# First image ahead of the weights, and a last projection split by heads, in an attention block on one core

## The chip, the cores and the metric

One NeuronCore of one Trainium2 chip runs the whole program. The metric is the device time of one execution in microseconds (us). Every run used here has a granted TensorE clock of 0.997 or more.

Engines are called as the profile calls them: PE is TensorE, PEld its weight loads, DVE VectorE, ACT ScalarE, POOL GpSimd, SPq and ACTq the queues that issue transfers. `rstd` is the reciprocal of the norm's standard deviation, one small power on GpSimd per image; it serves as a mark for the images.

## The reference, cut to what matters

Sixteen images of 512 channels and 32 x 32 = 1024 positions, in fp32, go through a group norm, a four-head attention over the positions, and a projection with a residual.

```python
def _L0_conv_ref(x, norm_gamma, norm_beta, qkv_w, qkv_b, proj_w, proj_b):
    NUM_HEADS, NUM_GROUPS, EPS = 4, 8, 1e-05
    b, c, h, w = x.shape            # 16, 512, 32, 32
    ...
    xn = ((xg - mu) * jax.lax.rsqrt(var + EPS)).reshape(b, c, h, w)
    xn = xn * norm_gamma[:, None, None] + norm_beta[:, None, None]
    qkv = jnp.einsum('oc,bchw->bohw', qkv_w, xn) + qkv_b[:, None, None]
    q, k, v = jnp.split(qkv, 3, axis=1)
    ...
    attn = jax.nn.softmax(jnp.einsum('bhnd,bhmd->bhnm', q, k) * scale, axis=-1)
    out = jnp.einsum('bhnm,bhmd->bhnd', attn, v)
    ...
    out = jnp.einsum('oc,bchw->bohw', proj_w, out) + proj_b[:, None, None]
    return x + out
```

## The kernel before

The three matrix products with weights (q and k, v, projection) are each done as 2 x 2 blocks with seven products in place of eight (Strassen's scheme in Winograd's form). For that, sums of weight blocks are formed once, and sums of image blocks (or of the heads' outputs) per image. `t1` to `t4` are the image sums, `s1` to `s4` the weight sums; s1, s2, s4 have buffers of their own, s3 overwrites a21, t1 overwrites b12.

```python
FACTORS = {
    1: ("a11", "b11"), 2: ("a12", "b21"), 3: ("s4", "b22"), 4: ("a22", "t4"),
    5: ("s1", "t1"), 6: ("s2", "t2"), 7: ("s3", "t3"),
}

def sums_of_a(eng, a, cols):          # weights
    for k in range(KC):
        def at(n):
            return a[n][k][:, cols]
        eng.tensor_add(at("s1"), at("a21"), at("a22"))
        eng.tensor_sub(at("s3"), at("a11"), at("a21"))
        eng.tensor_sub(at("s2"), at("s1"), at("a11"))
        eng.tensor_sub(at("s4"), at("a12"), at("s2"))

def sums_of_b(eng, b):                # image, or heads' outputs
    for k in range(KC):
        eng.tensor_sub(b["t3"][k], b["b22"][k], b["b12"][k])
        eng.tensor_sub(b["t1"][k], b["b12"][k], b["b11"][k])
        eng.tensor_sub(b["t2"][k], b["b22"][k], b["t1"][k])
        eng.tensor_sub(b["t4"][k], b["b21"][k], b["t2"][k])
```

One quad of products, `quad`, is a list of seven units, run in the order p1, p6, p2, p7, p5, p4, p3. Each unit is four matmul instructions and an eviction. Two accumulator banks (`ps_a`, `bufs=2`) serve them all.

```python
        def p6():
            mm(bank(6), 6, True)
            u[2] = upool.tile([P, HALF], F32, tag="u2", bufs=2, name=f"{name}_u2")
            nc.vector.tensor_add(u[2], banks[6], u["p1"])
        ...
        return [p1, p6, p2, p7, p5, p4, p3]
```

In the projection the residual is loaded into one of four `y` buffers (`ypool`, `bufs=4`), and for three of the four output blocks GpSimd adds it after the eviction:

```python
        def plus(which, half):
            def f(acc, u):
                t = upool.tile([P, HALF], F32, tag="yu", bufs=2, name=f"yu_{b}_{o}_{which}_{half}")
                nc.vector.scalar_tensor_tensor(t, acc, bias(which), u, ALU.add, ALU.add)
                nc.gpsimd.tensor_add(res[which, half], res[which, half], t)
                store(which, half)
            return f
```

The main loop has 8 steps per head. Beside the scores and weighted sums of a step, it emits what the plan of that head holds; in the fourth head that is the next image's norm, its image sums, the q/k quad of its first head and both v quads:

```python
        elif b + 1 < B:
            spread(plan, [lambda c=c: normalise(b + 1, c) for c in range(NCC)], 0, 1)
            plan[0].append(lambda: x_sums(b + 1))
            spread(
                plan, qk_units(b + 1, 0) + v_units(b + 1, 0) + v_units(b + 1, 1), 1, NB
            )
```

The start, with the v bias carried through the projection (32 one-column instructions), and the end:

```python
    load_x(0)
    ...                                   # wqk on the sync queue, wv and wp on ScalarE's
    stats_group(0)
    for half in range(NH2):
        for c in range(NCC):
            normalise(0, c, half)
    x_sums(0)
    sums_of_a(nc.vector, wqk, ts(0, P))
    sums_of_a(nc.gpsimd, wv, slice(0, HC))
    sums_of_a(nc.gpsimd, wqk, slice(P, C))
    for o in range(NCC):
        ...                               # acc[:, 0:1] += block.T @ vb_sb[:, c], added to projb_sb
    sums_of_a(nc.gpsimd, wp, slice(0, HC))
    for u in qk_units(0, 0) + v_units(0, 0) + v_units(0, 1):
        u()
    ...                                   # the main loop
    divide(B - 1, HEADS - 1)
    o_sums(B - 1)
    for u in proj_units(B - 1, 0) + proj_units(B - 1, 1):
        u()
```

The division needs one row of reciprocal totals on all partitions: `row` goes out to memory and `rinv` comes back broadcast, one transfer after the other.

## Time and profile before

| | before |
|---|---|
| time, median of the first 3 runs | 3400.59 us (3399.67 to 3401.64) |
| profiled span | 3400.3 us |
| TensorE busy | 3342.2 us, 98% |
| first q/k product, first v product | 35.62, 52.26 us |
| one image to the next (rstd to rstd), mean of 14 | 209.21 us |
| first projection product of the last image to the end of the span | 39.83 us |
| of it, until the last head's division starts | 7.63 us |

A profile row gives start, busy time, engine, line, operation, `output<-inputs`, shapes, count, and in brackets the idle time before it with what ended it. Busy time alone does not show where this program can be made faster, because TensorE is busy nearly everywhere; the gaps at the start, once per image and at the end do.

### The profile page before, as it was taken

Reading aid. Unit: us, or ns where it says so; the run is one execution under the profiler, and the core shown is the slowest. Engines: PE = TensorE matmul, PEld = TensorE weight load, DVE = VectorE, ACT = ScalarE, POOL = GpSimd, SP = SyncE. Lnnn points to the kernel's source line nnn. Section 1 sums busy time; section 2 is a strip of 40 time slices with the busy share of each in tenths; the row PEclk is TensorE's granted clock in tenths of the full one; section 3 lists DMA queues with packets and bytes.
Section 4 is the critical chain, followed back from the end, with each engine's and each line's share of the span. In section 5 each row is a group of like instructions: output and inputs, shape, how many; then the busy total and the mean of one; then the engine's idle time right before and its main releaser. Section 6 shows DMA issues by size and latency. Waiting matters only on the chain.

```text
span 3400.3 us, 22944 instructions
## 1 busy us (share of the span) xinstructions
PE 3342.2 (98%) x8674; PEld 1635.7 (48%) x8674; DVE 1641.3 (48%) x2408; ACT 790.8 (23%) x869; POOL 172.4 (5%) x140
## 2 busy tenths in 40 slices
PE   6999999999999999999999999999999999999998
PEld 4454454544545445454454545445454454544543
DVE  4454644546345464453544545454454544546444
ACT  1222222222122121221222212222222212222221
POOL 2000000000000000000000000000000000000000
PEclk9999999999999999999999999999999999999999
DMA  2001101011020110101111011110101101011011
GB/s 87 13 31 43 56 13 68 19 59 41 18 76 13 56 37 28 65 13 56 38 38 56 13 56 37 40 53 13 62 31 44 50 13 62 31 44 56 13 56 51
DMA packets 62660, 140.24 MB, mean 41 GB/s; under 512 B 10320, under 2 KB 12368, under 8 KB 62544
## 3 DMA queue, kind: packets, MB, share of 16 engines
q1 hardware_dynamic: 59232, 135.56, 11.4%
q10 hardware_dynamic: 3312, 3.16, 0.3%
q8 instruction: 70, 1.15, 0.1%
q14 instruction: 46, 0.38, 0.0%
HBM read 104.87 MB, written 33.82 MB: 41 GB/s over the span
## 4 chain that ended last, share of the span: by engine, by line
PE 63%; issue 29%; DVE 5%; POOL 2%; DMA 1%; ACT 0%; SPq 0%; POOLq 0%; DVEq 0%
PE po L489 15%; PE s L445 14%; PE qk L319 13%; PE pp L386 11%; PE v L352 11%; DVE x L71 1%; POOL rstd L63 1%; DVE xt L156 1%; DVE tt L462 1%; POOL y L417 1%; DVE part L464 1%; DMA wqk_a<-in_qkv_wT 0%; ACT p L450 0%; DVE yu L416 0%; DVE tot L455 0%
## 5 line engine op out<-in xcount | busy, mean ns | idle before, releaser
L450 ACT ACTIVATE p<-s 128x1024 f32<-128x1024 f32 x512 | 524.4, 1024 | 2031.4 <-PE s L445 2029.1
L489 PE MATMUL po<-p,v 128*128 128x512 f32 x2048 | 972.1, 593 | 0.0
L445 PE MATMUL s<-qk,qk 128*128 128x512 f32 x2048 | 964.8, 592 | 0.0
L455 DVE TENSOR_TENSOR tot<-tot,p 128x1024 f32<-128x1024 f32 x384 | 477.4, 1243 | 931.6 <-ACT p L450 931.0
L445 PEld LDWEIGHTS s<-qk,qk 128*128 128x128 f32 x2048 | 389.1, 190 | 489.4 <-issue 482.2
L489 PEld LDWEIGHTS po<-p,v 128*128 128x128 f32 x2048 | 386.8, 190 | 443.4 <-issue 388.8
L319 PE MATMUL qk<-x,wqk_a 128*128 128x512 f32 x512 | 248.4, 603 | 0.7 <-ACT qk_p L283 0.7
L319 PE MATMUL qk<-x,wqk_s 128*128 128x512 f32 x512 | 243.0, 592 | 0.0
L319 PE MATMUL qk<-xt,wqk_a 128*128 128x512 f32 x512 | 240.6, 592 | 0.0
L417 POOL TENSOR_TENSOR y<-y,yu 128x512 f32<-128x512 f32 x96 | 121.0, 1267 | 2232.2 <-DVE yu L416 2232.2
L498 DVE TENSOR_TENSOR o<-o,rinv 128x1024 f32<-128x1024 f32 x64 | 78.2, 1223 | 199.9 <-ACT o L495 139.4
L319 PEld LDWEIGHTS qk<-x,wqk_a 128*128 128x128 f32 x512 | 96.8, 192 | 130.1 <-issue 97.3
L336 DVE SCALAR_TENSOR_TENSOR qk<-qk,qkb_sb,qk_u 128x512 f32<-128x512 f32 x192 | 143.4, 747 | 28.7 <-PE qk L319 28.7
L319 PEld LDWEIGHTS qk<-xt,wqk_a 128*128 128x128 f32 x512 | 97.3, 190 | 122.5 <-issue 122.5
L319 PEld LDWEIGHTS qk<-x,wqk_s 128*128 128x128 f32 x512 | 97.3, 190 | 122.5 <-issue 122.0
L319 PE MATMUL qk<-xt,wqk_s 128*128 128x512 f32 x256 | 127.3, 610 | 17.9 <-DVE xt L158 17.9
L386 PE MATMUL pp<-o,wp_a 128*128 128x512 f32 x256 | 122.9, 602 | 5.1 <-DVE o L498 5.1
L386 PE MATMUL pp<-ot,wp_a 128*128 128x512 f32 x256 | 122.7, 602 | 0.0
L386 PE MATMUL pp<-o,wp_s 128*128 128x512 f32 x256 | 121.9, 598 | 0.0
L352 PE MATMUL v<-wv_a,xt 128*128 128x256 f32 x512 | 121.0, 379 | 0.0
L352 PE MATMUL v<-wv_a,x 128*128 128x256 f32 x512 | 120.9, 379 | 0.0
L352 PE MATMUL v<-wv_s,x 128*128 128x256 f32 x512 | 120.9, 379 | 0.0
(93 smaller groups left out, 2043.5 us busy)
## 6 DMA issues: line engine op xcount, KB each, us to landing
y<-in_x SPq DMA_DIRECT2D x128, 256.0 KB, 2.6
rinv<-row SPq DMA_DIRECT2D x64, 512.0 KB, 3.6
out_y<-y SPq DMA_DIRECT2D x128, 256.0 KB, 2.0
x<-in_x SPq DMA_DIRECT2D x62, 512.0 KB, 3.8
wqk_a<-in_qkv_wT SPq DMA_DIRECT2D x8, 256.0 KB, 4.5
x<-in_x ACTq DMA_DIRECT2D x2, 512.0 KB, 6.9
wv_a<-in_qkv_wT ACTq DMA_DIRECT2D x8, 128.0 KB, 4.1
wp_a<-in_proj_wT ACTq DMA_DIRECT2D x8, 128.0 KB, 4.1
```

Source lines behind the costliest of these rows:

```text
L63: nc.gpsimd.tensor_tensor(rstd, ve, self.neghalf, ALU.pow)
L71: nc.vector.tensor_scalar(xn, x, mu[:, c : c + 1], sc[:, c : c + 1], ALU.subtract, ALU.mult)
L319: nc.tensor.matmul(acc, wqk[wn][k][:, ts(h, P)], xb[b][xn][k], start=(first and k == 0), stop=(k == KC - 1), skip_group_check=True,)
L336: return lambda acc, u: nc.vector.scalar_tensor_tensor(dst(which, half), acc, bias(which), u, ALU.add, ALU.add)
L352: nc.tensor.matmul(acc[:, ts(g, HC)], xb[b][xn][k][:, ts(2 * jj + g, P)], wv[wn][k], start=(first and g == 0 and k == 0), stop=(k == KC - ...
L386: nc.tensor.matmul(acc, wp[wn][k][:, ts(o, P)], ob[b][on][k], start=(first and k == 0), stop=(k == KC - 1), skip_group_check=True,)
L417: nc.gpsimd.tensor_add(res[which, half], res[which, half], t)
L445: nc.tensor.matmul(sc[:, ts(half, HALF)], ks[b, h][:, ts(j, P)], qs[b, h][:, ts(half, HALF)], start=True, stop=True,)
L450: nc.scalar.activation(ps[s], sc, AF.Exp, scale=SCALE)
L455: nc.vector.tensor_add(tot[b, h], tot[b, h], ps[s])
L489: nc.tensor.matmul(po[b, h][:, ts(half, HALF)], vs[b, h // 2][:, h % 2, j, :], p[:, ts(half, HALF)], start=(j == 0), stop=(j == NB - 1),)
L498: nc.vector.tensor_mul(os_[b, h], os_[b, h], rinv.pop((b, h)))
```

## The change

Its intent is threefold. At the start, the first image must not wait for weight sums or bias products: GpSimd gets no work before the norm's power, weights come in one queue with the first head's columns first, small "warm" products keep TensorE active until the image is there, and the bias products move into the second head. In the middle, the image sums are reordered so that t2 is ready early, and the next image's units begin one step later. At the end, the products that don't need the last head run before its division, with four extra accumulator banks taken from the scores; the residual is added to `u` on VectorE, ahead of the last eviction. A new rule makes residual loads wait for the image's last eviction (`last_eviction`).

```diff
-def sums_of_b(eng, b):
-    for k in range(KC):
-        eng.tensor_sub(b["t3"][k], b["b22"][k], b["b12"][k])
-        eng.tensor_sub(b["t1"][k], b["b12"][k], b["b11"][k])
-        eng.tensor_sub(b["t2"][k], b["b22"][k], b["t1"][k])
-        eng.tensor_sub(b["t4"][k], b["b21"][k], b["t2"][k])
+def sums_of_b(eng, b, rows=(1, 2), chunks=range(KC)):
+    def sub(o, i, j):
+        for k in chunks:
+            eng.tensor_sub(b[o][k], b[i][k], b[j][k])
+    if 1 in rows:
+        sub("t1", "b12", "b11")
+    if 2 in rows:
+        sub("t2", "b22", "t1")
+        sub("t3", "t2", "b11")
+        sub("t4", "b21", "t2")
@@ loads (cut) @@
+    nc.scalar.activation(primer, ones, AF.Exp)
...
+    load_first()          # wqk, columns 0 to 127
+    load_v()
+    load_rest()           # wqk, the others
+    load_p()
@@ quad (cut): any order of units, banks may come from elsewhere @@
-            u["p1"] = upool.tile([P, HALF], F32, tag="p1", name=f"{name}_p1")
+            u["p1"] = upool.tile([P, HALF], F32, tag="p1", bufs=2, name=f"{name}_p1")
...
+            results.get("u2", nothing)(u[2])
@@ projection @@
+            tc.add_manual_dep(
+                dma.ins, last_eviction[b].ins.name,
+                mybir.DependencyInfo(mybir.DependencyClass.Sync, mybir.DependencyReason.DATA),
+                reason="residual",
+            )
...
+        def add(u, *places):
+            for at in places:
+                eng.tensor_add(res[at], res[at], u)
+        def put(which, half):
+            def f(acc, u=None):
+                t = res.pop((which, half))
+                bias = projb_sb[:, o + 2 * which : o + 2 * which + 1]
+                nc.vector.scalar_tensor_tensor(t, acc, bias, t, ALU.add, ALU.add)
+                nc.sync.dma_start(out[b, ts(o + 2 * which, P), ts(half, HALF)], t)
             return f
@@ plan of the fourth head @@
-                plan, qk_units(b + 1, 0) + v_units(b + 1, 0) + v_units(b + 1, 1), 1, NB
+                plan, qk_units(b + 1, 0) + v_units(b + 1, 0) + v_units(b + 1, 1), 2, NB
@@ start @@
+    before_power = norm.last
+    warm(9, "warm")
...
-    sums_of_a(nc.vector, wqk, ts(0, P))
-    sums_of_a(nc.gpsimd, wv, slice(0, HC))
-    sums_of_a(nc.gpsimd, wqk, slice(P, C))
...
+    with tc.issue_after(before_power.ins):
+        sums_of_a(nc.vector, wqk, ts(0, P))
+    for u in qk_units(0, 0, order=(1, 2, 6, 7, 5, 4, 3)):
+        u()
+    sums_of_a(nc.vector, wv, slice(0, HC))
+    for u in v_units(0, 0) + v_units(0, 1):
+        u()
@@ end @@
-    divide(B - 1, HEADS - 1)
-    o_sums(B - 1)
-    for u in proj_units(B - 1, 0) + proj_units(B - 1, 1):
+    order = (1, 5, 2, 6, 7, 4, 3)
+    first = proj_units(B - 1, 0, nc.vector, order=order, home={6: home(6, 0), 7: home(6, 1)})
+    second = proj_units(B - 1, 1, nc.vector, order=order, home={1: home(1, 0), 5: home(1, 1)})
+    sums_of_b(nc.vector, ob[B - 1], (1,))
+    for u in first[:1] + second[:1] + first[1:2] + second[1:2]:
+        u()
+    sums_of_b(nc.vector, ob[B - 1], (2,), (0,))
+    divide(B - 1, HEADS - 1)
+    sums_of_b(nc.vector, ob[B - 1], (2,), (1,))
+    for u in first[2:3] + second[2:3] + first[3:] + second[3:]:
         u()
```

More of the change, by code (lines that the diff above doesn't have):

```diff
@@ L60, in group @@
         ve = gn.tile([P, k], F32, tag="ve", name="ve")
-        nc.vector.tensor_scalar_add(ve, pv[:, :k], EPS)
+        self.last = nc.vector.tensor_scalar_add(ve, pv[:, :k], EPS)
         rstd = gn.tile([P, k], F32, tag="rstd", name="rstd")
@@ L202, in fast_path @@
     load_x(0)
+    primer = wpool.tile([BLK, 1], F32, name="primer")
+    nc.vector.memset(ones, 1.0)
+    nc.scalar.activation(primer, ones, AF.Exp)
     nc.vector.memset(avg, 0.0)
@@ L206, in fast_path, with w_tiles @@
     nc.vector.memset(neghalf, -0.5)
-    nc.vector.memset(ones, 1.0)
-    for t, src in ((gamma_sb, gamma), (beta_sb, beta), (qkb_sb, qk_b)):
+    for t, src in (
+        (gamma_sb, gamma), (beta_sb, beta), (qkb_sb, qk_b), (vb_sb, v_b), (projb_sb, proj_b)
+    ):
         nc.scalar.dma_start(t, src)
-    def w_tiles(name, cols, dma, blocks):
+    def w_tiles(name, cols, blocks, parts):
         w = {}
@@ L216, in w_tiles, with load @@
         w["s3"] = w["a21"]
-        for n, src in blocks:
-            for k in range(KC):
-                dma.dma_start(w[n][k], src[ts(k, P), :])
-        return w
+        def load(part):
+            for n, src in blocks:
+                for k in range(KC):
+                    nc.sync.dma_start(w[n][k][:, part], src[ts(k, P), part])
+        return w, [lambda part=part: load(part) for part in parts]
     def blocks_of(first, second):
@@ L226, in blocks_of @@
         ]
-    wqk = w_tiles("wqk", C, nc.sync, blocks_of(qkv_wT[:, 0:C], qkv_wT[:, C : 2 * C]))
-    wv = w_tiles(
-        "wv", HC, nc.scalar,
+    wqk, (load_first, load_rest) = w_tiles(
+        "wqk", C, blocks_of(qkv_wT[:, 0:C], qkv_wT[:, C : 2 * C]), (slice(0, P), slice(P, C))
+    )
+    wv, (load_v,) = w_tiles(
+        "wv", HC,
         blocks_of(qkv_wT[:, 2 * C : 2 * C + HC], qkv_wT[:, 2 * C + HC : 3 * C]),
+        (slice(0, HC),),
     )
-    nc.scalar.dma_start(vb_sb, v_b)
-    nc.scalar.dma_start(projb_sb, proj_b)
-    wp = w_tiles("wp", HC, nc.scalar, blocks_of(proj_wT[:, 0:HC], proj_wT[:, HC:C]))
+    wp, (load_p,) = w_tiles(
+        "wp", HC, blocks_of(proj_wT[:, 0:HC], proj_wT[:, HC:C]), (slice(0, HC),)
+    )
+    load_first()
+    load_v()
+    load_rest()
+    load_p()
     norm = Norm(nc, gn, ps_a, avg, neghalf, gamma_sb, beta_sb, NCC, N)
@@ L268, in x_sums, with quad @@
         sums_of_b(nc.vector, xb[b])
-    def quad(name, mm, results, shape=None):
-        banks = {}
+    def quad(name, mm, results, order=(1, 6, 2, 7, 5, 4, 3), home=None):
+        banks, u = {}, {}
+        nothing = lambda u: None
         def bank(i):
-            banks[i] = ps_a.tile([P, HALF], F32, tag="acc", name=f"{name}_{i}")
+            if home and i in home:
+                banks[i] = home[i]()
+            else:
+                banks[i] = ps_a.tile([P, HALF], F32, tag="acc", name=f"{name}_{i}")
             return banks[i]
@@ L295, in p7 @@
             mm(bank(7), 7, True)
-            u[3] = upool.tile([P, HALF], F32, tag="u3", name=f"{name}_u3")
+            u[3] = upool.tile([P, HALF], F32, tag="u3", bufs=2, name=f"{name}_u3")
             nc.vector.tensor_add(u[3], banks[7], u[2])
+            results.get("u3", nothing)(u[3])
+            if 5 in banks:
+                results["c22"](banks[5], u[3])
         def p5():
             mm(bank(5), 5, True)
-            results["c22"](banks[5], u[3])
+            if 3 in u:
+                results["c22"](banks[5], u[3])
         def p4():
@@ L309, in p3, with qk_units @@
             results["c12"](banks[5], u[2])
-        u = {}
-        return [p1, p6, p2, p7, p5, p4, p3]
-    def qk_units(b, h):
+        units = {1: p1, 2: p2, 3: p3, 4: p4, 5: p5, 6: p6, 7: p7}
+        return [units[i] for i in order]
+    def qk_units(b, h, **kw):
         def mm(acc, i, first):
@@ L342, in qk_units @@
             "c12": plus(0, 1), "c21": plus(1, 0), "c22": plus(1, 1),
-        })
+        }, **kw)
     def v_units(b, jj):
@@ L379, in o_sums, with proj_units @@
         sums_of_b(nc.vector, ob[b])
-    def proj_units(b, o):
+    def proj_units(b, o, eng, **kw):
         def mm(acc, i, first):
@@ L395, in load @@
             t = ypool.tile([P, HALF], F32, tag="y", name=f"y_{b}_{o}_{which}_{half}")
-            nc.sync.dma_start(t, x[b, ts(o + 2 * which, P), ts(half, HALF)])
-            res[which, half] = t
-        def store(which, half):
-            nc.sync.dma_start(
-                out[b, ts(o + 2 * which, P), ts(half, HALF)], res.pop((which, half))
-            )
-        def bias(which):
-            return projb_sb[:, o + 2 * which : o + 2 * which + 1]
-        def c11(acc):
-            nc.vector.scalar_tensor_tensor(
-                res[0, 0], acc, bias(0), res[0, 0], ALU.add, ALU.add
-            )
-            store(0, 0)
-        def plus(which, half):
-            def f(acc, u):
-                t = upool.tile([P, HALF], F32, tag="yu", bufs=2, name=f"yu_{b}_{o}_{which}_{half}")
-                nc.vector.scalar_tensor_tensor(t, acc, bias(which), u, ALU.add, ALU.add)
-                nc.gpsimd.tensor_add(res[which, half], res[which, half], t)
-                store(which, half)
+            dma = nc.sync.dma_start(t, x[b, ts(o + 2 * which, P), ts(half, HALF)])
+            tc.add_manual_dep(
+                dma.ins, last_eviction[b].ins.name,
+                mybir.DependencyInfo(mybir.DependencyClass.Sync, mybir.DependencyReason.DATA),
+                reason="residual",
+            )
+            res[which, half] = t
+        def add(u, *places):
[7 more added lines that the diff above has]
+                nc.sync.dma_start(out[b, ts(o + 2 * which, P), ts(half, HALF)], t)
             return f
         units = quad(f"pp_{b}_{o}", mm, {
-            "c11": c11, "c12": plus(0, 1), "c21": plus(1, 0), "c22": plus(1, 1),
-        })
+            "u2": lambda u: add(u, (0, 1), (1, 0)), "u3": lambda u: add(u, (1, 1)),
+            "c11": put(0, 0), "c12": put(0, 1), "c21": put(1, 0), "c22": put(1, 1),
+        }, **kw)
         first = units[0]
@@ L432, in proj_units @@
         return [with_loads] + units[1:]
-    ps, tot, po, rinv = {}, {}, {}, {}
+    ps, tot, po, rinv, last_eviction = {}, {}, {}, {}, {}
     def where(s):
@@ L494, in weighted_sum @@
             os_[b, h] = opool.tile([P, N], F32, tag="o", name=f"o_{b}_{h}")
-            nc.scalar.copy(os_[b, h], po.pop((b, h)))
+            last_eviction[b] = nc.scalar.copy(os_[b, h], po.pop((b, h)))
     def divide(b, h):
@@ L503, in spread, with bias_of_v @@
             plan[first + i * (last - first) // len(units)].append(u)
+    def bias_of_v(o):
+        acc = ps_a.tile([P, HALF], F32, tag="acc", name=f"pb_{o}")
+        half, oo = divmod(o, 2)
+        for c in range(NCC):
+            block = wp[f"a{half + 1}{c // KC + 1}"][c % KC]
+            nc.tensor.matmul(
+                acc[:, 0:1], block[:, ts(oo, P)], vb_sb[:, c : c + 1],
+                start=(c == 0), stop=(c == NCC - 1),
+            )
+        nc.vector.tensor_add(
+            projb_sb[:, o : o + 1], projb_sb[:, o : o + 1], acc[:, 0:1]
+        )
     def plan_head(b, h):
         plan = [[] for _ in range(NB)]
+        if b == 0 and h < 2:
+            if h == 0:
+                plan[0].append(lambda: sums_of_a(nc.vector, wqk, ts(1, P)))
+                plan[3].append(lambda: sums_of_a(nc.vector, wqk, ts(2, P)))
+            else:
+                plan[0].append(lambda: sums_of_a(nc.vector, wqk, ts(3, P)))
+                spread(plan, [lambda o=o: bias_of_v(o) for o in range(NCC)], 1, 5)
+                plan[6].append(lambda: sums_of_a(nc.vector, wp, slice(0, HC)))
         if h == 0:
@@ L511, in plan_head @@
                 plan[3].append(lambda: o_sums(b - 1))
-                spread(plan, proj_units(b - 1, 0), 4, NB)
+                spread(plan, proj_units(b - 1, 0, nc.gpsimd), 4, NB)
         elif h == 1:
             if b > 0:
-                spread(plan, proj_units(b - 1, 1), 0, 4)
+                spread(plan, proj_units(b - 1, 1, nc.gpsimd), 0, 4)
             spread(plan, qk_units(b, 2), 0, NB)
@@ L526, in plan_head, with warm @@
             spread(
-                plan, qk_units(b + 1, 0) + v_units(b + 1, 0) + v_units(b + 1, 1), 1, NB
+                plan, qk_units(b + 1, 0) + v_units(b + 1, 0) + v_units(b + 1, 1), 2, NB
             )
         return plan
+    def warm(n, name):
+        acc = ps_s.tile([P, N], F32, tag="s", name=name)
+        for _ in range(n):
+            ins = nc.tensor.matmul(acc[:, :P], avg, avg, start=True, stop=True)
+            tc.keep_in_program_order(ins)
     for c in range(NCC):
@@ L537, in fast_path @@
     x_sums(0)
-    sums_of_a(nc.vector, wqk, ts(0, P))
-    sums_of_a(nc.gpsimd, wv, slice(0, HC))
-    sums_of_a(nc.gpsimd, wqk, slice(P, C))
-    for o in range(NCC):
-        acc = ps_a.tile([P, HALF], F32, tag="acc", name=f"pb_{o}")
-        half, oo = divmod(o, 2)
-        for c in range(NCC):
-            block = wp[f"a{half + 1}{c // KC + 1}"][c % KC]
-            nc.tensor.matmul(
-                acc[:, 0:1], block[:, ts(oo, P)], vb_sb[:, c : c + 1],
-                start=(c == 0), stop=(c == NCC - 1),
-            )
-        nc.vector.tensor_add(
-            projb_sb[:, o : o + 1], projb_sb[:, o : o + 1], acc[:, 0:1]
-        )
-    sums_of_a(nc.gpsimd, wp, slice(0, HC))
-    for u in qk_units(0, 0) + v_units(0, 0) + v_units(0, 1):
+    with tc.issue_after(before_power.ins):
[4 more added lines that the diff above has]
+    for u in v_units(0, 0) + v_units(0, 1):
         u()
@@ L582, in fast_path, with home, f @@
     nc.vector.tensor_scalar(flag, fine, -1.0, 1.0, ALU.mult, ALU.add)
+    spare = {}
+    def home(i, half):
+        def f():
+            if i not in spare:
+                spare[i] = ps_s.tile([P, N], F32, tag="s", name=f"spare_{i}")
+            return spare[i][:, ts(half, HALF)]
+        return f
+    ob[B - 1] = halves([os_[B - 1, h] for h in range(HEADS)], "o")
+    order = (1, 5, 2, 6, 7, 4, 3)
[5 more added lines that the diff above has]
+    sums_of_b(nc.vector, ob[B - 1], (2,), (0,))
     divide(B - 1, HEADS - 1)
-    o_sums(B - 1)
-    for u in proj_units(B - 1, 0) + proj_units(B - 1, 1):
+    sums_of_b(nc.vector, ob[B - 1], (2,), (1,))
+    for u in first[2:3] + second[2:3] + first[3:] + second[3:]:
         u()
```

## The prediction

> **What bounds the kernel now.** I read three views in this order. First the page's busy times and its 40 slices, to see how much any change can win.
>
> ```profile
> PE 3342.2 (98%) x8674; PEld 1635.7 (48%) x8674; DVE 1641.3 (48%) x2408; ACT 790.8 (23%) x869; POOL 172.4 (5%) x140
> ...
> PE   6999999999999999999999999999999999999998
> ```
>
> TensorE (PE) is busy 98% of the span, and only the first and the last slice (85 us each) fall below 9 tenths. Part of this is busy time that need not be so long, so I set up a floor from the spacing of instruction starts instead. In the timeline of the middle, four 512-column instructions start every 1.715 us (0.4288 each), eight 256-column ones every 1.717 us (0.2146 each). There are 2048 + 2048 + 1792 + 896 = 6784 of the first kind (lines 445, 489, 319, 386; each product is four) and 1792 of the second (line 352): 2909 + 385 us. The small products of norm and bias add about 8: 3302 us. The change removes none of this; all that can be won is 3400 - 3302 = 98 us, or 2.9%. So "faster by over 2%" (68 us) would need two thirds of all that is not product time.
>
> Second, the waits of TensorE between 62 and 3360 us: one line.
>
> ```profile
> PE qk L319 <- DVE xt L158: 17.9, 15, 1.2
> ```
>
> Once in each of 15 images TensorE waits 1.2 us for the second sum of the next image. From one image to the next 209.2 us pass (the rstd of image after image starts at 193.24, 402.45, 611.66); the floor of an image is 424 x 0.4288 + 112 x 0.2146 = 205.8. Of the 3.4 us between, summing the gaps beyond those spacings over one image gives 1.35 at this wait; the rest is ten-odd gaps of 0.1 at changes between streams and 0.3 for the norm's products.
>
> Third, the timelines of the start and of the end.
>
> ```profile
> 13.80 0.16 DVE L61 TENSOR_SCALAR ve<-pv 128x4 f32<-128x4 f32 x1 [0.68 <-PE pv L59]
> ...
> 15.89 0.72 POOL L147 TENSOR_TENSOR wv_s<-wv_a,wv_a 128x256 f32<-128x256 f32 x1 [15.44 <-DMA wv_a<-in_qkv_wT]
> 16.57 1.02 POOL L63 TENSOR_TENSOR rstd<-ve,neghalf 128x4 f32<-128x4 f32 x1
> ...
> 18.34 7.51 DVE L71 TENSOR_SCALAR x<-x,mu,sc 128x512 f32<-128x512 f32 x8
> ...
> 23.24 5.01 ACT L75 ACTIVATE x<-x,beta_sb 128x512 f32<-128x512 f32 x8
> ...
> 27.79 1.08 DVE L148 TENSOR_TENSOR wqk_a<-wqk_a,wqk_a 128x128 f32<-128x128 f32 x1
> ...
> 30.79 0.28 DVE L150 TENSOR_TENSOR wqk_s<-wqk_a,wqk_s 128x128 f32<-128x128 f32 x1
> ...
> 32.19 3.58 PE L547 MATMUL pb<-vb_sb,wp_a 128*128 128x1 f32 x16 [8.81 <-DVE projb_sb L551]
> ...
> 35.62 3.76 PE L319 MATMUL qk<-x,wqk_a 128*128 128x512 f32 x4
> ```
>
> The norm has its variance at 14.0, but GpSimd (POOL) took a weight sum first that waited for its load, so rstd ends at 17.6. Then eight scalings take 0.94 us each on VectorE (DVE), weight sums on it 1.08 instead of 0.28, and the bias products stand in front of the first q/k product, which starts at 35.6. The v products start at 52.26.
>
> ```profile
> 3360.47 1.88 PE L386 MATMUL pp<-o,wp_a 128*128 128x512 f32 x4
> ...
> 3368.10 1.23 DVE L498 TENSOR_TENSOR o<-o,rinv 128x1024 f32<-128x1024 f32 x1 [3.48 <-DMA rinv<-row]
> ...
> 3369.38 2.07 PE L386 MATMUL pp<-o,wp_a 128*128 128x512 f32 x2 [5.12 <-DVE o L498]
> ...
> 3394.26 1.26 POOL L417 TENSOR_TENSOR y<-y,yu 128x512 f32<-128x512 f32 x1 [0.45 <-DVE yu L416]
> ```
>
> At the end only 8 of 56 projection instructions run before the last head's division; TensorE idles 5.1 us for it, then does the other 48. From the last GpSimd add (ends 3395.5) to the end of the span are 4.8 us: store and close.
>
> **What the Trainium skill says.** "TensorE: Matmul & The Clock Gate", Part 1, has TensorE at half clock until some 3.4 us of activity have passed, and again after an idle window. The trace agrees in size: products after idle start every 0.85 us at 40 us and every 0.43 from 44, and 0.85 again at 3373; so the idle at the end costs about 2.5 us more than itself. "SBUF — State Buffer", Who interferes with whom: VectorE instructions with two SBUF inputs and reading GpSimd ones exclude each other. The trace agrees: 1.08 us for a 128x128 sum beside GpSimd, 0.28 after. "DMA: Bandwidth & Descriptors", Issuing engines are not separate DMA queues: all issues share 16 engines, so one queue costs no bandwidth. The trace has 411 to 414 GB/s from 4 to 8 us with two queues, and 393 in the best 2 us of a later image load from one. "ScalarE: Activation LUTs", What ACT_TABLE_LOAD costs, gives 1.28 us for a load; the one here took 1.28 at 21.94, on the path.
>
> **The change, part by part.**
>
> *Start.* The image's loads and statistics stay as they are: variance at 14.0. GpSimd has nothing before rstd now: 1.0 us at the first image's duration, 1.9 at the later ones', so it ends by 16. Meanwhile VectorE does the eight first-column weight sums (8 x 0.28 = 2.3, to 16.3). Scalings without GpSimd beside them: 128x1024 takes 0.735 in the row of a later image, so I estimate 0.42 per half; first half done by 18.2, second by 20. ScalarE (ACT) adds beta behind at 0.63 each (5.01 / 8), its table loaded early: first half by 19.5, second by 22. TensorE, kept busy by nine small products, starts p1 at 18.2 and p2 after it to 21.6, then p6 once t2 is there (two t1, then t2, 0.69 each: 22.1 and 22.8), then p7, p5, p4, p3 at 1.715: done at about 31. Before: 52.3. Gain 21. Against it: the 32 bias instructions, formerly ahead of it all, now take TensorE's full-clock time, at about 0.11 each (half of 3.58 / 16): 3.5. The sums for v (8 of 128x256, some 0.42 each) and the later weight sums move from GpSimd to VectorE, which has slack; I allow 2 us of waits. **Start: 16 us, 11 to 19.**
>
> *Middle.* The units of the next image begin two steps into the fourth head, not one: one pass of scores and weighted sum (3.43 us) more for VectorE; and t2 is complete after four of the eight sums, where it was the seventh. The wait should go: 15 x 1.35 = 20 us at most. ScalarE's betas hold up exp there, and 21 units now share six steps, so I take 17. **Middle: 17 us, 10 to 21.** The residual adds stay three per projection on GpSimd (1.27 each), only on u; the VectorE count is the same. No change.
>
> *End.* Before the division TensorE can do p1 and p5 of both outputs (16 instructions, 6.9 us from 3360.5) and head 2's part of p2: it is busy until the division is done at 3369.3, so it neither idles nor cools. With no wait at all 56 x 0.43 = 24 us would end at 3384.5, against 3393.3. But VectorE has, after the division, three sums (2.1) and per output 5 x 0.69 + 4 x 0.75 = 6.45: 15 us, to 3384.4, as long as TensorE. And there are four residual buffers: the second output's loads (2.6 us) wait for the first's stores (2.0 us). The first's c12 store leaves at about 3380.3, so the second's load of that place lands near 3385, and u is added there. End of the last add near 3388 to 3391 instead of 3395.5. **End: 6 us, 3 to 9.**
>
> Sum: 16 + 17 + 6 = 39, so 3361 us. A check from below: 18.2 (first product) + 3302 + 15 x 2.0 (other gaps of an image) + 4 (waits at start and end) + 6 (last add, store, close) = 3360. I say 3361.
>
> **Rivals.** (a) *The wait in the middle stays or moves*: the x sums take the same 5.5 us of VectorE, whose queue also holds the transposes, norm and exp totals; denser units may then wait for accumulators (there are two). For it: the gap is 1.2 us and VectorE was continuously busy around it. Against: 3.4 us of room, and the dense stretch 52 to 61 ran without a gap. It would leave 3372 to 3378. (b) *VectorE becomes the bound at the end*, or its queue stops at an add whose residual has not landed: the end then gives 0 to 3, so 3364 to 3367. (c) *The weight loads are hidden anyway, and the start is bound by VectorE*: if the first-column weights come late in the one queue, the sums placed before the scalings hold these up. The image and all weights are some 6.3 MB; at the 283 GB/s of the first 26 us they take 22 us, but the first 2.6 MB should have landed by 11. A late load would cost 3 to 5: 3365. (d) *Everything works to the floor*: 3352.
>
> **Range and chances.** The three parts are independent and each is uncertain by 3 to 5; together about 7, some more for the unknown order of instructions: 3349 to 3375 for 8 in 10. All of it lies inside 2% (3333 to 3469): same 0.98, faster 0.01, slower 0.01.
>
> **What would show it.** First q/k product near 18 us and first v product near 31; rstd directly after the variance; no table load on the path; bias products some 3.5 us in the second head. In the middle 207.2 to 208 us per image and no 1.2 us wait for xt. At the end no wait of 5 us for the division, TensorE ending about 3385 to 3390 less what was won before, and VectorE waiting for a residual load or GpSimd absent. The prediction is wrong if a new wait recurs per image (15-fold), or if the first products wait for weights.

## More of the kernel before

The chain of waits follows the last work backwards. These are two links of it at the end of the kernel before (start, us, what):

```profile
3363.31 1.32 DMA row<-r
...
3364.70 3.31 DMA rinv<-row
```

The division of the last head hangs on these two transfers, 4.6 us together; no residual load is issued near them.

## The result, and the profile after

| | before | after |
|---|---|---|
| time, median of 6 runs | 3401.64 us (3399.67 to 3403.27) | 3372.81 us (3370.82 to 3373.80) |
| ratio | | 0.9915 (0.9902 to 0.9928): same, within 2% |
| profiled span | 3400.3 us | 3368.8 us |
| first q/k product | 35.62 | 17.41 |
| first v product | 52.26 | 32.96 |
| from there to the second image's rstd | 140.98 | 144.56 |
| second to sixteenth rstd | 2928.91 | 2916.67 |
| sixteenth rstd to the last image's first projection product | 238.32 | 237.17 |
| from there to the end of the span | 39.83 | 37.44 |

A ratio is the mean time of one kernel's runs over the mean of the other's runs of the same rounds, so it is not quite the ratio of the medians. The last five rows of the table, from the first v product on, add up to the span. The profiled run of the changed kernel is its fastest one, 2 us below the median; that matters below.

The prediction was 3361 us in a range of 3349 to 3375. The time is inside the range, at its slow side: 28.8 us were won where 39.6 were predicted.

The page of the changed kernel, busy times and TensorE's 40 slices:

```profile
PE 3334.8 (99%) x8692; PEld 1634.4 (49%) x8692; DVE 1632.5 (48%) x2454; ACT 790.7 (23%) x870; POOL 141.9 (4%) x110
...
PE   8999999999999999999999999999999999999998
```

The first slice rose from 6 to 8 tenths; 18 more TensorE instructions (the nine warm products are two instructions each) did not raise its busy time, which fell by 7 us, nearly all of it before the first v product, where fewer products run at half clock.

What TensorE waits for in the changed kernel (us in total, times, longest):

```profile
PE qk L351 <- DVE qk_u L315: 5.5, 15, 0.4
PE spare L418 <- DVE y L445: 4.0, 1, 4.0
PE qk L351 <- DVE qk L368: 2.2, 2, 1.2
PE qk L351 <- DMA wqk_a<-in_qkv_wT: 2.0, 1, 2.0
```

The wait of 1.2 us for an image sum, 15 times, is gone. In its place there is one of 0.4, again 15 times, for an eviction on VectorE, and one of 1.0 and 1.2 us in two of the images. The single wait of 4.0 us is at the end. The last line is at the start: the instruction there starts at 21.25 us, just as VectorE has made the first t2, which it also needs, so I put this wait down to t2 and not to the transfer that the profile names.

The timeline of the start:

```profile
14.11 1.02 POOL L63 TENSOR_TENSOR rstd<-ve,neghalf 128x4 f32<-128x4 f32 x1 [13.65 <-DVE ve L61]
...
15.46 3.73 DVE L71 TENSOR_SCALAR x<-x,mu,sc 128x512 f32<-128x512 f32 x8
16.03 5.01 ACT L75 ACTIVATE x<-x,beta_sb 128x512 f32<-128x512 f32 x8 [12.37 <-DMA wv_a<-in_qkv_wT]
...
17.41 1.88 PE L351 MATMUL qk<-x,wqk_a 128*128 128x512 f32 x4
...
24.53 0.28 DVE L149 TENSOR_TENSOR wqk_s<-wqk_s,wqk_a 128x128 f32<-128x128 f32 x1
...
25.83 1.02 PE L351 MATMUL qk<-xt,wqk_s 128*128 128x512 f32 x2
...
32.96 1.89 PE L384 MATMUL v<-wv_a,x 128*128 128x256 f32 x8
```

GpSimd takes the power at once, the eight scalings take 3.73 us instead of 7.51, and the first product follows 2 us after the first of them. The first half of p6 runs at 21.25, the second only at 25.83: the weight sum it needs, at 24.53, stood on VectorE behind eight image sums.

The timeline of the end:

```profile
3331.36 1.88 PE L418 MATMUL pp<-o,wp_a 128*128 128x512 f32 x4
...
3332.60 0.81 SPq L428 DMA_DIRECT2D y<-in_x  x2
...
3334.21 0.33 SPq L503 DMA_DIRECT2D row<-r  x1
...
3341.13 1.23 DVE L527 TENSOR_TENSOR o<-o,rinv 128x1024 f32<-128x1024 f32 x1 [5.70 <-DMA rinv<-row]
...
3358.06 0.69 DVE L439 TENSOR_TENSOR y<-y,pp_u 128x512 f32<-128x512 f32 x1 [1.58 <-DMA y<-in_x]
...
3361.05 2.71 PE L418 MATMUL spare<-o,wp_s 128*128 128x512 f32 x4 [3.99 <-DVE y L445]
...
3363.80 0.75 DVE L445 SCALAR_TENSOR_TENSOR y<-spare,projb_sb,y 128x512 f32<-128x512 f32 x1 [2.81 <-PE spare L418]
```

And the links of its chain of waits that answer to those shown of before:

```profile
3334.21 1.86 DMA row<-r
...
3336.13 4.90 DMA rinv<-row
...
3354.68 3.30 DMA y<-in_x
```

Two of the first output's residual loads are now issued at 3332.60, ahead of `row`, and two more between `row` and `rinv`, because the new rule holds them until the last eviction. The row took 1.86 us instead of 1.32 and its way back 4.90 instead of 3.31; the division starts 9.77 us after the first projection product, not 7.63. Then, 17 us later, VectorE stops for a residual of the second output, whose buffers came free late; TensorE waits 4.0 us for a bank, and its last four instructions take 2.71 us instead of the 1.88 that four take in the first row.

### The profile page after: what moved, and what is told of

It reads as the page before. It is cut to its first block, busy times and chain, and to the rows that moved or that the text cites. A ratio compares the mean times of both kernels' runs of the same rounds, so it can differ in the third digit from the quotient of the medians.

```text
span 3368.8 us, 23014 instructions
## 1 busy us (share of the span) xinstructions
PE 3334.8 (99%) x8692; PEld 1634.4 (49%) x8692; DVE 1632.5 (48%) x2454; ACT 790.7 (23%) x870; POOL 141.9 (4%) x110
## 3 DMA queue, kind: packets, MB, share of 16 engines
q8 instruction: 70, 1.15, 0.1%
q10 hardware_dynamic: 1008, 1.06, 0.1%
## 5 line engine op out<-in xcount | busy, mean ns | idle before, releaser
L484 DVE TENSOR_TENSOR tot<-tot,p 128x1024 f32<-128x1024 f32 x384 | 470.1, 1224 | 920.5 <-ACT p L479 920.0
L439 POOL TENSOR_TENSOR y<-y,pp_u 128x512 f32<-128x512 f32 x90 | 112.7, 1266 | 1882.6 <-DVE pp_u L315 1758.5
L445 DVE SCALAR_TENSOR_TENSOR y<-pp,projb_sb,y 128x512 f32<-128x512 f32 x124 | 92.7, 748 | 120.6 <-PE pp L418 99.8
```

What stands on the lines that cost most here:

```text
L439: eng.tensor_add(res[at], res[at], u)
L445: nc.vector.scalar_tensor_tensor(t, acc, bias, t, ALU.add, ALU.add)
L484: nc.vector.tensor_add(tot[b, h], tot[b, h], ps[s])
```

## The experiments

All of them gave correct results. Times are medians; "per image" is the distance of one rstd to the next, taken in the profile, as the median over the images. The kernel before, run again beside them, had 3402.97 us (first group), 3402.62 (second), 3403.10 (third) and 3401.74 (the last run).

### The middle: which part does what

My theory was that both the new order of the sums and the later start were needed, and that a backlog on VectorE would take over as the wait; the rival, that one of them does it all, or that other parts of the change (second buffers, moved loads) matter. The first three kernels put only these parts into the kernel before.

**order_only** has the new `sums_of_b` alone:

```diff
-        eng.tensor_sub(b["t3"][k], b["b22"][k], b["b12"][k])
-        eng.tensor_sub(b["t1"][k], b["b12"][k], b["b11"][k])
-        eng.tensor_sub(b["t2"][k], b["b22"][k], b["t1"][k])
-        eng.tensor_sub(b["t4"][k], b["b21"][k], b["t2"][k])
+    sub("t1", "b12", "b11")
+    sub("t2", "b22", "t1")
+    sub("t3", "t2", "b11")
+    sub("t4", "b21", "t2")
```

> The kernel before, with only the order of the sums of the next image changed (t2 is complete after four of eight sums, not seven). Theory: the 1.2 us wait per image for the second sum is lateness of t2; three sums of 0.69 us earlier is 2.1 us, more than the 1.2 wait, so the wait of the q/k products for this sum falls from 17.9 us to under 3 us and an image takes 208.0 to 208.3 us instead of 209.2. Rival: the sums wait for ScalarE's normalised halves and for VectorE's queue, so the order alone gains little and an image stays above 208.8.

It took 3392.60 us (one run), 208.64 us per image: a miss, half of the expected gain. The new order brings t2 forward in VectorE's queue, but t2 needs the last chunks of the image too. In the third image ScalarE ends the fourth chunk's beta at 408.37 us, VectorE takes the t2 sums at 408.49, after a reduction of 1.21 us in between, and TensorE has its first one at 409.22.

**shift_only** starts the units one step later, and nothing else:

```diff
-                plan, qk_units(b + 1, 0) + v_units(b + 1, 0) + v_units(b + 1, 1), 1, NB
+                plan, qk_units(b + 1, 0) + v_units(b + 1, 0) + v_units(b + 1, 1), 2, NB
```

> The kernel before, with only the units of the next image begun at step two instead of one of the fourth head. Theory: 3.4 us of room is more than the 1.2 us wait, so the wait goes with this too and an image takes 208.0 to 208.3 us; a new wait of about 0.4 us for the u2 add (VectorE's queue has the exp totals in front of it) appears as in the changed kernel. Rival: the old order of sums keeps t2 late and leaves a part of the wait, above 208.5.

It took 3394.99 us (one run), 208.90 per image, also a miss: the rival ("above 208.5") held. **order_shift** has both edits:

> The kernel before with both changes to the middle, nothing at the start and the end. Theory: the stages add up, so this gives what the middle gave in the changed kernel: 208.1 us per image, 13 us in all, 3387 to 3389 us. Rival: the middle's gain in the changed kernel came partly from the residual added to u or the moved residual loads; then an image takes over 208.5 here.

It took 3391.84 us, ratio 0.9968 (0.9951 to 0.9985), 208.51 per image: slower than the expected 208.1 and 3387 to 3389 us, at the edge of the rival's "over 208.5". The waits of TensorE once per image, in order_only, shift_only and order_shift:

```profile
PE qk L322 <- DVE xt L157: 10.8, 15, 0.7
```

```profile
PE qk L319 <- DVE xt L158: 3.0, 15, 0.2
PE qk L319 <- DVE qk_u L288: 2.5, 15, 0.2
```

```profile
PE qk L322 <- DVE qk_u L291: 5.5, 15, 0.4
```

Each edit alone shortens the wait for the sum, from 1.2 to 0.7 or to 0.2. The two together remove it, and the wait for the eviction `qk_u`, absent before, takes 0.4. So the new wait does not come from anything else in the change: these two edits in the old kernel reproduce it to the tenth. They are worth 0.70 of the 1.08 us per image that the changed kernel wins (209.21 to 208.13); 0.38 must come from elsewhere. The traces show where it lies: order_shift has four gaps of about 0.1 us in the second head, 139 to 142 us after an image's rstd, where q/k and projection products begin, and the changed kernel has none there.

**spread3** starts the units another step later in the changed kernel, which should cure a backlog:

```diff
-                plan, qk_units(b + 1, 0) + v_units(b + 1, 0) + v_units(b + 1, 1), 2, NB
+                plan, qk_units(b + 1, 0) + v_units(b + 1, 0) + v_units(b + 1, 1), 3, NB
```

> The changed kernel with the units of the next image begun at step three instead of two (21 units in five steps). Theory: what remains of the wait (0.37 us on the u2 add per image) comes from VectorE's backlog of norm, sums, transposes and totals at the start of the head; two totals later it is worked off, so the wait goes and an image takes 207.5 to 207.8 us, 5 to 9 us less in all. Rival: the wait comes from the units standing close together on two accumulators; closer still, it stays or grows, and the time is the same or up to 10 us more.

It took 3360.72 us, ratio 0.9875 (0.9859 to 0.9892): 12.1 us less than the changed kernel, with 207.50 per image, as the theory had it. The 0.63 us per image are the gap at that wait (0.53 beyond the normal spacing in the traces) and the slower step after it (0.11). The whole is more than the expected 5 to 9, as the two slow images went too. No wait of TensorE recurs per image, and none of 1.2 us is left in the later images. So the backlog was the cause of what remained, and the denser units (21 in five steps) did no harm.

**bufs1** takes back the second buffers of `p1` and `u3`:

```diff
-            u["p1"] = upool.tile([P, HALF], F32, tag="p1", bufs=2, name=f"{name}_p1")
+            u["p1"] = upool.tile([P, HALF], F32, tag="p1", name=f"{name}_p1")
...
-            u[3] = upool.tile([P, HALF], F32, tag="u3", bufs=2, name=f"{name}_u3")
+            u[3] = upool.tile([P, HALF], F32, tag="u3", name=f"{name}_u3")
```

> The changed kernel with one buffer each for the p1 copy and for u3, as before the change, instead of two. An image takes 208.13 us in the changed kernel and 208.51 with only the two changes to the sums; the residual loads are not the cause (the run without their rule stays at 208.13). Theory: the 0.38 us come from the residual added to u (no VectorE add and buffer in between), so an image stays at 208.1. Rival: they come from the second buffers, so it goes to 208.4 to 208.6.

It took 3373.86 us (one run), 208.13 per image, as the changed kernel: the second buffers are worth nothing per image. At the end they do matter: without them TensorE has fewer products to run before the division and waits 3.8 us for it, not 1.0, and the products after it are at half clock (0.85 us apart). The kernel **nodep** below has 208.14, so neither are the moved residual loads. What remains for the 0.38 us is the residual that is added to `u`, off the path of the evictions. That is by elimination; no run undid this part alone, though the place of the gaps, beside the projection, fits it.

### The end: the residual's loads

My theory was that the loads cost twice: their new place ahead of `row` delays the division, and four buffers make the second output's loads wait for the first output's stores. The rival was that the VectorE work after the division, some 15 us, bounds the end whatever the loads do.

**nodep** drops the new rule, so the first output's residuals are loaded as early as before:

```diff
-            tc.add_manual_dep(
-                dma.ins, last_eviction[b].ins.name,
-                ...
-                reason="residual",
-            )
```

> The changed kernel without the rule that a residual is loaded only after the last weighted sum of its image; the loads go as soon as a buffer is free. Theory: at the end the four residual loads stood in front of the row and rinv transfers in the same queue and made these 1.86 and 4.90 us instead of 1.32 and 3.31; without them the division starts 7.6 us after the first projection product instead of 9.8, so the end is about 2 us shorter (35.4 instead of 37.4 us). Rival: the row and rinv transfers are slow there for another reason (TensorE's products of both outputs, chance), then nothing changes. Middle: an image stays at 208.1 if the 0.38 us that the changed kernel gains over the two changes to the sums comes from u, and goes to 208.5 if it came from the moved loads.

It took 3369.89 us, ratio 0.9904 (0.9888 to 0.9921). The division starts 8.14 us after the first projection product, 1.63 earlier than with the rule:

```profile
3340.16 1.22 DVE L522 TENSOR_TENSOR o<-o,rinv 128x1024 f32<-128x1024 f32 x1 [4.06 <-DMA rinv<-row]
```

The end took 35.08 us instead of 37.44, but TensorE still waits 3.9 us for the last bank, as the second cost is untouched.

**second_x** keeps the rule and gives the second output's residuals room of their own: in the last image the four buffers of the next image's input lie idle, so its residuals are loaded there, whole rows, at the start of the last head.

```diff
+    def residual_in_x(o):
+        for which in range(2):
+            t = xpool.tile([P, N], F32, tag="x", name=f"yx_{o}_{which}")
+            nc.sync.dma_start(t, x[B - 1, ts(o + 2 * which, P), :])
+            early[o, which] = t
...
-        elif b + 1 < B:
+        elif b + 1 == B:
+            plan[0].append(lambda: residual_in_x(1))
+        else:
```

> The changed kernel with the residuals of the second output of the last image in two tiles of the image that are free by then, loaded during the last head; the first output's loads stay as they are. Theory: the second output waits for residual buffers that the first output's stores give free (waits of TensorE of 4.0 us and of VectorE of 1.6 and 0.8 us); without that the last product follows at once and the end is 4 to 6 us shorter (31.5 to 33.5 instead of 37.4). Rival: VectorE's own adds (about 13 us after the division) are the bound at the end; then it is under 2 us.

It took 3365.21 us, ratio 0.9890 (0.9874 to 0.9907). The end took 31.62 us, with the division as late as in the changed kernel (9.98 us). VectorE no longer stops for a residual, and TensorE no longer waits for a bank; its last four instructions follow at once:

```profile
3355.76 1.88 PE L427 MATMUL spare<-o,wp_s 128*128 128x512 f32 x4
```

So the wait for the buffers cost some 6 us by the profiles (7.6 by the medians), more than the delayed division.

**tail_x** does the same for both outputs, so that no residual load is near the end:

```diff
+            plan[0].append(lambda: residual_in_x(0))
+            plan[0].append(lambda: residual_in_x(1))
```

> As the last, with the residuals of both outputs in the four image tiles. Theory: both costs go, 6 to 8 us, the end takes 29.5 to 31.5 us and the whole 3365 to 3367. Rival: the 2 us of the transfers before the division are hidden again by the products that run in the meantime, then it is like the last.

It took 3363.56 us, ratio 0.9884 (0.9868 to 0.9901). From the timeline of its end:

```profile
3339.98 1.23 DVE L539 TENSOR_TENSOR o<-o,rinv 128x1024 f32<-128x1024 f32 x1 [4.00 <-DMA rinv<-row]
...
3354.70 1.88 PE L427 MATMUL spare<-o,wp_s 128*128 128x512 f32 x4
3356.62 0.75 DVE L457 SCALAR_TENSOR_TENSOR yx<-spare,projb_sb,yx 128x512 f32<-128x512 f32 x1 [0.97 <-PE spare L427]
```

The last four instructions take 1.88 us: TensorE neither waited nor cooled. The end took 30.39 us, 7.05 less than in the changed kernel's profile and 9.4 less than before. TensorE is on its chain of waits from end to end, so VectorE was not the bound: that rival fell. So did the rival of this run: with the division 1.9 us earlier the end is 1.2 us shorter than in second_x (1.65 us by the medians). The whole time came out 1.4 us below its expected range. With early loads, the split of the last projection was worth what I had hoped and more; the late loads gave it back.

### The start: what won the 19 us

Theory: the first product came early because VectorE had no reading GpSimd beside it, and TensorE was fast because the warm products had released its clock. Rivals: only the order of the sums matters; or the warm products could as well be the bias products, which would save the 3.6 us they take later.

**nowarm** drops the warm products:

```diff
-    warm(9, "warm")
```

> The changed kernel without its nine warming products. Theory: the clock is then at half when the first q/k product starts at 17.4 us, and in the run with the bias products in their place it stayed at half up to 30 us, so the first v product starts 3 to 6 us later than 33.0 and the time is 3375 to 3379. Rival: the q/k products wait for VectorE's sums there anyway, then it is under 1 us.

It took 3373.54 us, ratio 0.9913 (0.9898 to 0.9928). The v products start at 34.62 us instead of 32.96, a loss of 1.7 where my theory had 3 to 6. From its timeline:

```profile
16.61 3.78 PE L351 MATMUL qk<-x,wqk_a 128*128 128x512 f32 x4 [2.97 <-ACT x L75]
```

The first four instructions do run at half clock: 3.78 us, where the eight profiles with warm products have 1.88 to 2.74 (only in the changed kernel's own and in best3's was the clock released before the first of them). So the warm products work. But the products after them wait for sums in any case, so most of the loss falls into a wait. In the whole time no loss is resolved: 0.9913 against the changed kernel's 0.9915, with the intervals nearly equal.

**pool_sums** puts the sums that moved to VectorE back on GpSimd, but behind the power, so that only the contention returns and not the delay of rstd:

```diff
         sums_of_a(nc.vector, wqk, ts(0, P))
+    sums_of_a(nc.gpsimd, wv, slice(0, HC))
+    sums_of_a(nc.gpsimd, wqk, slice(P, C))
...
-    sums_of_a(nc.vector, wv, slice(0, HC))
```

> The changed kernel with the weight sums of v and of the other q/k columns back on GpSimd, but behind the norm's rstd in its queue. Theory: of the 19 us won up to the first v product, a part is that VectorE no longer shares its read port with GpSimd: the eight scalings take about 7 us again instead of 3.7 and the sums that overlap 1.0 us instead of 0.28 and 0.69, so the first v product starts at 37 to 42 us instead of 33. Rival: only the place of rstd behind a sum that waits for its load counted; then it starts at 33 to 34.

It took 3383.07 us, ratio 0.9941 (0.9926 to 0.9957). The v products start at 41.97 us, 9.0 later than in the changed kernel. From its timeline:

```profile
15.29 5.79 DVE L71 TENSOR_SCALAR x<-x,mu,sc 128x512 f32<-128x512 f32 x8
...
23.99 2.88 DVE L158 TENSOR_TENSOR xt<-x,x 128x512 f32<-128x512 f32 x2
```

The scalings take 5.79 us for eight (3.73 without GpSimd beside them), an image sum 1.44 us (0.64 without). So 9 of the 19.3 us won at the start are VectorE's, freed from GpSimd's reading; the other 10 are, by subtraction, what the rest of the new start gives: the earlier rstd and the bias products out of the way.

**bias_early** puts the 32 bias instructions in place of the warm ones, with the projection weights loaded early for them:

```diff
     load_first()
+    load_p()
     load_v()
     load_rest()
-    load_p()
...
-    warm(9, "warm")
+    pb = bias_of_v()
...
+    nc.vector.tensor_add(projb_sb, projb_sb, pb[:, 0:NCC])
```

> The changed kernel with the 32 bias instructions in place of the nine warming products (all in one bank), and the weights of the projection loaded second in the queue. Theory: the bias cost 3.5 us of TensorE's full-clock time in the second head (from the first v product to the second image's norm 144.6 us instead of 141.0); here they stand where TensorE has nothing else and warm it as well, so the span falls 2 to 3.5 us. Rival: the projection weights come too late or the products stay at half clock and push the first q/k product back by as much; then nothing is gained.

It took 3372.29 us, ratio 0.9908 (0.9891 to 0.9924): no gain. The stretch to the second image's rstd shrank from 144.56 to 140.98, so the bias products had cost exactly 3.58 us there. But the v products start at 38.09, 5.1 later. From its timeline:

```profile
13.41 4.08 PE L541 MATMUL pb<-vb_sb,wp_a 128*128 128x1 f32 x18
17.35 2.05 PE L351 MATMUL qk<-x,wqk_a 128*128 128x512 f32 x2
...
25.60 3.62 PE L351 MATMUL qk<-x,wqk_a 128*128 128x512 f32 x4
```

Eighteen one-column instructions take as long as the 18 warm ones of 128 columns did (3.88 us), yet the q/k products after them still run at 0.9 to 1.0 us each, even at 25.60. One-column products didn't release the clock; the rival held. The clock is not all of the 5.1 us: nowarm, with no warming at all, lost only 1.7, and here the other 14 bias instructions ran among the q/k products, 3.0 us in all.

### A version that beats both

**best3** takes spread3 and tail_x together, keeps the warm products, and mends the two faults that were left at the start: the first head's weight sums go ahead of the image sums, and the bias products fill a gap between the first q/k products, once the clock has been released (the rewriting of `bias_of_v` is cut here, as above).

```diff
     load_first()
+    load_p()
     load_v()
     load_rest()
-    load_p()
...
-    x_sums(0)
     with tc.issue_after(before_power.ins):
         sums_of_a(nc.vector, wqk, ts(0, P))
+    x_sums(0)
     for u in qk_units(0, 0, order=(1, 2, 6, 7, 5, 4, 3)):
         u()
+    pb = bias_of_v()
+    nc.vector.tensor_add(projb_sb, projb_sb, pb[:, 0:NCC])
```

> Everything that helped in one kernel: the changed kernel with the next image's units from step three, the last image's residuals in its image tiles, the first weight sums put ahead of the image sums, the warming products kept, and the bias products put between the first q/k products (projection weights loaded second). Theory: gains add: 12 (middle) + 7 (end) + 3.6 (bias out of the second head) + 0 to 1: 3349 to 3353. Rival: the one-column bias products let the clock fall to half at the start again, as in their run, and cost 3 to 6 us there: 3353 to 3359.

It took 3349.25 us (3348.37 to 3352.72, five runs), ratio 0.9847 (0.9833 to 0.9860) to the kernel before. That is in the expected range, and some 24 us below the changed kernel. From its start:

```profile
19.38 3.63 PE L553 MATMUL pb<-vb_sb,wp_a 128*128 128x1 f32 x32
...
22.86 1.96 PE L351 MATMUL qk<-x,wqk_a 128*128 128x512 f32 x4
```

The bias products lie in a gap that was there anyway: the first v product is at 33.25, as in the changed kernel, and the second image's rstd 140.98 us later, 3.58 sooner. The four products after them start 0.43 us apart, so the clock was not lost over these one-column products. That they keep it is not shown: an idle stretch of 2.94 us in bufs1 didn't lose it either, one of 3.76 did. All waits of TensorE in the whole of best3 are these two, both in the first image's norm:

```profile
PE pm L48 <- DVE mean L46: 11.8, 1, 11.8
PE pv L59 <- DVE vv L57: 0.8, 1, 0.8
```

## Why the prediction was right, and where its sizes were off

The class and the range held. The class was nearly given by the ceiling of 98 us; the sizes of the three parts are the real test. Taken from the profiles:

| part | predicted | measured | of what |
|---|---|---|---|
| start | 16 (11 to 19) | 15.7 | v products 19.30 earlier, less 3.58 for the bias in the second head |
| middle | 17 (10 to 21) | 13.4 | 12.24 from the second to the sixteenth rstd, 1.15 in the last image |
| end | 6 (3 to 9) | 2.4 in the profiled run, about 0.6 on average | see below |

**The start was right in size and mechanism.** The first q/k product came at 17.41 (18.2 predicted), rstd directly after the variance, and the table load was off the path. The first v product came at 32.96, not 31. The scalings took 0.47 us each instead of the estimated 0.42. And the step "p6 once t2 is there" left out a term: p6 needs the weight sum s2 as well, whose second chunk stood on VectorE behind the image sums until 24.53, and so p6's second half came at 25.83. best3, which turns the two kinds of sums round, fits 3.6 us of bias products in and still has its first v product at 33.25. So the v products came 19.3 us earlier, where 21 were predicted; the 2 us that the prediction allowed for waits made up for it, without naming this one. The bias products cost 3.58 us, 3.5 predicted. pool_sums shows that the contention was rightly named, although the prediction's line for a sum of 0.28 us "after" GpSimd was one that ran between two of GpSimd's sums, which went on to 38.45. Rival (c) did not come: the first-column weights had landed by 12.36 us, ahead of the variance. That one queue costs no bandwidth was not shown, though: from 8 to 12 us the changed kernel moved 128 GB/s, the kernel before 362, and no run separates the queue from the smaller pieces.

**The middle was right in mechanism, and a little too large in size.** The wait for the sum went, as predicted. Rival (a), that it moves, came true at a third of its size: 0.4 us for VectorE's backlog, 15 times, which order_shift reproduces and spread3 removes. Per image 208.13 us were measured where 17 / 15 us below 209.21 make 208.08. So the size was right for most images; two of them took 209.38 and 209.65, some 2.8 us more together, and that is most of the rest. In these two TensorE waits 1.0 and 1.2 us for an eviction, behind a division that had waited for its row. In spread3 no such image is left; why the row came late in just these two was not tested.

**The end is the term that was mis-sized.** The step that failed is the sum under *End*: "The first's c12 store leaves at about 3380.3, so the second's load of that place lands near 3385, and u is added there. End of the last add near 3388 to 3391 instead of 3395.5." The chain of store and load was foreseen, but four of its terms were too small or missing. Put into the time frame of before (by the first projection product), they are:

- The division was assumed to start as before, and started 2.1 us later (9.77 instead of 7.63): residual loads in front of `row` and `rinv`. nodep gives 1.6 of it back; the rest is within the scatter of the kernels without such loads (7.6 to 8.2).
- The residual landed at 3387 in that frame (3358.06 - 3331.36 + 3360.47), where the prediction had 3385.
- What follows it was taken as 3 to 6 us. It was 6.5 (3358.06 to 3364.55): two adds and two evictions in turn free a bank, and only then the last product runs. The prediction counted no product behind the late residual.
- That product loses the full clock after the wait: its first three instructions still start 0.53 and 0.43 us apart, the last alone takes 1.06 us, and the four 2.71. "It neither idles nor cools" held nearly at the division, where TensorE now waits 1.0 us, and failed 19 us later.

The last add ends at 3394 in that frame, instead of the 3388 to 3391. tail_x removes all four and ends in 30.39 us.

The profiled run flatters the end. In the four other profiles with this end unchanged (spread3, bias_early, nowarm, pool_sums) it takes 38.9 to 39.8 us; the mean of all five is 39.1. Four profiles with the old end have 38.9 to 40.4, mean 39.7. So the end gave about 0.6 us, and rival (b), 0 to 3 us "or its queue stops at an add whose residual has not landed", describes it. Then 15.7 + 13.4 + 0.6 = 29.7 us meets the 28.8 of the medians. In the slower profiles TensorE idled 4.3 to 4.9 us before its last four instructions, and these took 3.1 to 3.8; after 3.99 us of idling they took 2.71, after 3.91 (nodep) 2.42 and after 2.94 (bufs1) 1.98. That accounts for a part of the scatter. The rest lies before them (they start 0.4 to 0.9 us later) and behind them (last eviction, store and close take 5.4 to 6.5 us instead of 5.0); its cause is open.

## What to carry to other kernels

When TensorE is busy 98%, look for gaps by stage, and size a change by the wait that ends last in each; then ask what will run behind a transfer that comes late, not only when it comes. A transfer on the critical path should find its queue and its engines empty: load what is not urgent long before or after it, and at the end of a program use buffers that no next iteration needs. A wait that returns in every iteration can be worth as much as the start or the end: one step of slack in the schedule gave 12 us here, the new start 15.7.

## What the Trainium skill lacked or had wrong

- "TensorE: Matmul & The Clock Gate", Part 1, counts the warm-up in time, some 3.4 us, "not a number of matmuls", and gives no measure of how busy TensorE must be in it. Here 18 instructions of 128 columns in 3.88 to 4.19 us released the clock before or within the next four products (1.88 to 2.74 us), in eight profiles; 18 of one column in 4.08 us did not: the products after them were still 0.9 to 1.0 us each.
- "DMA: Bandwidth & Descriptors", the opening table, has some 358 GB/s as the limit of HBM per core, without the condition that a later section of the page gives, that both cores of the pair stream. With this one core running, the image's loads moved at 407 GB/s (4 to 8 us of the changed kernel, 413 before).
- No page that I used says how much a transfer on the critical path suffers from others issued just ahead. With two and four residual loads of 256 KB issued just ahead, the last `row` took 1.78 to 2.05 us and the last `rinv` 4.86 to 5.16 in seven profiles; without them 1.31 to 1.32 and 3.31 to 3.89 in the seven others.
